# Decoder layers on one Trainium2 core: one run of sums with v per batch, and moved transposes

## The chip, the cores and the metric

The kernel runs on one core of a Trainium2 chip. A core has a matrix engine (TensorE, "PE" in the profile, its weight loads "PEld"), a vector engine (VectorE, "DVE"), a scalar engine (ScalarE, "ACT"), a general engine (GpSimd, "POOL") and an engine that issues DMAs (SyncE, "SP"). Each engine works through its own list of instructions in order and waits on semaphores for the others. [...] The metric is the device time of one execution in microseconds (us). The kernel before has a median of 1778.74 us over three runs, from 1775.16 to 1784.4.

## The reference, cut to what matters

The input `x` is 8 batches of 256 positions of 256 numbers. Six post-norm decoder layers with causal linear attention (16 heads of 16) come first; a cross-attention with a difference of two softmaxes and a three-cycle gated FFN follow. The change touches only the six layers:

```python
for l in range(N_LAYERS):
    q = (x @ Wq[l] + bq[l]).reshape(Bx, Lx, N_HEADS, dh)
    k = (x @ Wk[l] + bk[l]).reshape(Bx, Lx, N_HEADS, dh)
    v = (x @ Wv[l] + bv[l]).reshape(Bx, Lx, N_HEADS, dh)
    a = causal_linear_attn(feature_map(q), feature_map(k), v)
    a = a.reshape(Bx, Lx, dm) @ Wo[l] + bo[l]
    x = x + a
    y = x = layer_norm(x, g1[l], be1[l])
    y = jax.nn.gelu(y @ W1[l] + b1[l], approximate=False) @ W2[l] + b2[l]
    x = layer_norm(x + y, g2[l], be2[l])
```

`feature_map` is `elu + 1`. Written out, the attention is, for each head, the masked product of scores `q k^T` with v (`x` is flipped, so in the original order a query sees the keys at and after its own position), divided by the sum of the masked scores.

## The kernel before, in words

Every batch and layer is cut into four stages, each a Python generator. `stage_q` transposes the batch's `x` (`to_T`), splits it into a high and a low part (`xTh` by ScalarE, `xTl` by VectorE), and projects q, k and v. Each product is made of three passes (high by high, high by low, low by high), six matmuls of 128x256 for each half of an output (`mm3`). The two halves of q are written to the two halves of one PSUM tile, `ps[:, m, :]`, and after each half ScalarE reads it out with the bias (L436); k likewise; v is read by VectorE when both halves are there (L453).

`stage_s` makes the scores. Its first round takes keys of the first 128 positions for all heads, its second and third rounds (`m` = 0 and 1, eight heads each) the keys of the last 128 positions. Each score matmul uses 32 rows of the array, and four of them run beside each other. VectorE masks the first round while reading it out (L505); ScalarE copies the others to `stk` (L521) and POOL masks those (L524). The sums with v (`av`) then use 128 rows and 17 columns: 16 values and one column of ones, which gives the denominator. Four heads are placed on four column groups of the array. One `av(m, ...)` is 16 calls of `mm`, which the trace shows as 32 matmuls. Before, `av` for `m` = 0 and for `m` = 1 are two separate runs into the same bank `av_bank`, each read out by ScalarE (L512) before the next may begin. The result is transposed back (L533) and divided (L537, L538).

`stage_w` projects the attention output, adds the residual and normalizes (`affine`, L345 and L351 on VectorE). `stage_f` transposes `xr` again and runs the FFN: four pieces of W1 with GELU on ScalarE (L596), their split into high and low parts, four pieces of W2.

PSUM has a tag for each purpose: `q` with four banks, `h` with two, `o` and `av` with one each. A new tile of a tag waits for the readers of the tile that had its bank.

The order of the work is written out by hand through due times. A stage yields a number before each step: its due time, in units of one batch (G is a sixteenth of it). `run_tasks` keeps all stages in a heap and runs the step that is due first, so one batch's steps come between those of others. A new batch starts each unit; stages start at `T_S`, `T_W` and `T_F` after it. The lists `Q_T`, `S_T`, `S_F`, `W_T` and the number `X_T` hold the due times inside a stage. `mm` and `tp` chain every TensorE instruction to the one before (`follow("pe", ...)`), so TensorE runs in exactly the order of due times. On the other engines a planner with a timeline of its own places the instructions, bound by data and by a few chains (`follow("dm", ...)`). Weight loads are issued on SP four weights ahead, and VectorE splits each loaded weight into two parts (`wprep`, L216 and L217) in the stage of the last batch of a layer.

Of the kernel before, what the change touches and what calls it, by code (L numbers as in the profile page):

```python
# [30 lines left out]
G = 1 / 16  # L31
T_S = 11.58 * G
T_W = 24.5 * G
T_F = 34 * G
Q_T = (2.6 * G, 3 * G, 4 * G, 5 * G, 6 * G, 7 * G, 7.6 * G, 8.2 * G, 8.8 * G)
S_T = (0.0, 2.02 * G, 6.06 * G, 5.0 * G, 7.12 * G)
S_E = 0.9 * G
S_F = (9.92 * G, 10.52 * G, G)
U_O = (1.5, 2.0, 5.0)
U_B0 = 10.0  # L40
UH = 7.4
# [11 lines left out]
FFP = 3.1  # L53
F_O = (1.45, 2.0, 2.85, 7.6, 11.4, 14.5)
W_T = (3.12 * G, 4.5 * G, 5.5 * G, 8 * G)
X_T = 1.58 * G
F_P = 0.16
W_P = 1
M_W = 1
# [34 lines left out]
def decoder_kernel(ctx: ExitStack, tc: tile.TileContext, A, out, nlay=NLAY, groups=GROUPS):  # L94
# [42 lines left out]
    def mm(o, **kw):  # L137
        ins = pe.matmul(o, **kw)  # L138
        if ORD:
            follow("pe", ins)  # L140
# [140 lines left out]
    def b2col(l, c):  # L281
        return bcol[:, 48 + l * 2 + c:49 + l * 2 + c]

    def bocol(l, c):
        return bcol[:, 60 + l * 2 + c:61 + l * 2 + c]
# [135 lines left out]
    def stage_q(w, b, k, last):  # L421

        l = w % nlay
        yield X_T
        xh, xl = yield from to_T(xr[b], None if w == 0 and b in groups[0][:3] else lambda c: bocol(l, c), t0=X_T)
        yield Q_T[0]
        xs = [(xh[:, c, :], xl[:, c, :]) for c in range(2)]
        q2 = S("stq", [P, 2, 2, 256], F32, 4)
        kf = T2("kf", 5)
        us_, es = (q2[:, 0], kf), []  # L430
        for a, kind in enumerate("qk"):
            wh, wl = W[kind, w, 0]
            ps = PS()
            for m in range(2):
                mm3(ps[:, m, :], [(wh[:, c, half(m)], wl[:, c, half(m)]) for c in range(2)], xs)
                act.activation(us_[a][:, m, :], ps[:, m, :], AF.Identity, bias=bqk1[:, a, l, m:m + 1])  # L436
                yield Q_T[1 + 2 * a + m]
            if last:
                wprep(kind, w + 1)
            e = T2("qe", 2)  # L440
            act.activation(e, us_[a], AF.Relu, scale=-1.0, bias=one)
            es.append(e)
        wh, wl = W["v", w, 0]
        ps = PS()
        va = vaug[k % 3]
        for t in range(2):
            mm3(ps[:, t, :], [(xh[:, c, half(t)], xl[:, c, half(t)]) for c in range(2)],
                [(wh[:, c, :], wl[:, c, :]) for c in range(2)], late="w")
            yield Q_T[5 + t]
        for a in range(2):  # L450
            table_op(act.activation(es[a], es[a], AF.Exp, scale=-1.0))  # L451
        vr = gb["v", w].rearrange("p t (h m) -> p t h m", m=16)
        dve.tensor_tensor(va[:, :, :, 0:16], ps.rearrange("p t (h m) -> p t h m", m=16), vr, ALU.add)  # L453
        if last:
            wprep("v", w + 1)
            rload("v", w + 1)
        yield Q_T[7]
        follow("dm", dve.tensor_tensor(es[0], es[0], us_[0], ALU.max))
        for e in range(2):
            pool.tensor_scalar(q2[:, e], es[0], eo[:, e:e + 1], 1.0, ALU.mult, ALU.mult)  # L460
        yield Q_T[8]
        follow("dm", dve.tensor_tensor(kf, kf, es[1], ALU.max))
        st[b] = dict(v=va, q=q2, k=kf)
# [12 lines left out]
    def stage_s(w, b, k):  # L476
# [1 line left out]
        d = st[b]  # L478
        va, q2, kf = d["v"], d["q"], d["k"]
        avs = S("avs", [P, 4, 256])  # L480
        o = av_bank

        def scores(o4, m, jt):
            n = 256 if jt else P
# [1 line left out]
                r = slice(32 * g, 32 * g + 32)  # L486
                mm(o4[g].rearrange("p (e n) -> p e n", e=2), lhsT=kf[r, m, half(jt)], rhs=q2[r, :, m, 0:n], start=True, stop=True)

        def av(m, a1, a0):
            for s in range(2):  # L490
                for jt in (1, 0):
                    for c in range(4):
                        g, e, n = 2 * s + c // 2, c % 2, 256 if jt else P
                        r = a1[g // 2][:, g % 2, e, :] if jt else a0[g][:, m, half(e)]
                        mm(o[32 * c:32 * c + 17, s, 0:n], lhsT=va[:, jt, 8 * m + 4 * s + c, :], rhs=r,
                           start=jt == 1, stop=jt == 0, tile_position=(0, 32 * c))

        yield S_T[0]
# [5 lines left out]
        for g in range(4):  # L504
            follow("dm", dve.tensor_tensor(a0[g].rearrange("p m (e n) -> p (m e) n", e=2), ps[g].rearrange("p m (e n) -> p (m e) n", e=2), maskT4, ALU.mult))  # L505
        a1s = []

        def second(m):
            yield S_T[2 + 2 * m]
            av(m, a1s[m], a0)  # L510
            yield S_T[2 + 2 * m] + S_E
            act.activation(avs[:, 2 * m:2 * m + 2, :], o, AF.Identity, bias=epc)  # L512

        for m in range(2):
            yield S_T[1 + 2 * m]
            ps = [PS("q") for g in range(4)]
            scores([flat(p) for p in ps], m, 1)
            yield S_T[1 + 2 * m] + S_E
            a1 = [S("stk", [P, 2, 2, 256], F32, 4) for i in range(2)]
            for g in range(4):  # L520
                act.copy(a1[g // 2][:, g % 2], ps[g])  # L521
            for g in range(4):
                x = a1[g // 2][:, g % 2, :, P:256]
                pool.affine_select(x, x, [[0, 2], [-1, P]], ALU.is_ge, 0.0, base=0, channel_multiplier=1)  # L524
            a1s.append(a1)
        for m in range(2):
            yield from second(m)
        ot = T2("hf", 3)
        for t in range(2):
            yield S_F[0] + S_F[2] * t  # L530
# [33 lines left out]

    def stage_f(w, b, k, last):
        l = w % nlay
        xh, xl = yield from to_T(xr[b], lambda c: b2col(l, c), "h")
        xs = [(xh[:, c, :], xl[:, c, :]) for c in range(2)]
        hs = {}
        order = [(1, 0), (1, 1), (1, 2), (2, 0), (1, 3), (2, 1), (2, 2), (2, 3)]  # L570
# [641 lines left out]
```

## Time and profile before

| | |
|---|---|
| median of three runs | 1778.74 us |
| profiled execution | 1775.11 us, span 1773.4 us |
| mean granted clock of TensorE | 0.988 |
| busy: PE / DVE / ACT / POOL | 1689.7 / 1288.3 / 1176.3 / 832.2 us |
| matmuls `p_av<-stk,vaug` (128 rows, 17 columns, 256 moving) | 1536, 387 ns each |
| score copies L521 on ACT | 384, 599 ns each |
| q and k reads L436 on ACT | 192, 475 ns each |
| transposes of xr into p_q / p_h | 224 / 216, 279 and 287 ns in the mean of the layers' form |

A line of the timeline gives the start, the length of a merged group of like instructions, the engine, the line of the code, the operation with its output and inputs, and the number of instructions; square brackets hold idle time before it and what ended that. Matmuls overlap, so the cost of a group is read from its start to the start of the next group and not from its length. An idle time is shown only where the engine's record is empty; a matmul that is held while the one before it still drains shows as a longer distance between starts. Groups are by tile: `p_q<-xTh,wah` is a projection of q or k, `p_q<-wah,xTh` one of v, `p_av<-stk,vaug` sums with v of the last 128 keys, `p_av<-a,vaug` of the first 128, `p_o<-w2h,hh` the second FFN matrix, `p_q<-stq,kf` scores.

### The profile page before, as it was taken

To read this page: it belongs to the slowest core of one execution; us is meant where nothing else is said; L and a number is where in the kernel's file an instruction comes from. 1 tells how busy PE (TensorE), PEld (TensorE's weight loads), DVE (VectorE), ACT (ScalarE), POOL (GpSimd) and SP (SyncE) were. 2 spreads that over 40 slices of the span, in tenths; PEclk is the share of its full clock that TensorE was granted. 3 is DMA by queue.
4 is the path that set the end of the run, shared out by engine and by line. 5 is a ranking of instruction groups with operands and counts; after the bars stand their busy time and mean duration, and the time that the engine had idled before them with its cause. 6 is when DMAs were issued, how large, how long until landed. Compare 5 with 4: busy or idle time off the path is not lost.

```text
span 1773.4 us, 38405 instructions
## 1 busy us (share of the span) xinstructions
PE 1689.7 (95%) x14992; PEld 1345.6 (76%) x14992; DVE 1288.3 (73%) x2846; ACT 1176.3 (66%) x2300; POOL 832.2 (47%) x1295
## 2 busy tenths in 40 slices
PE   6999999999999999999999999999988899999897
PEld 4688887888878888888888887888866555554795
DVE  5566777767777678766787677876668899886586
ACT  3556665666666766666666666666655788877687
POOL 7344444344434444443434434444556666643453
PEclk8999999999999999999999999999999999999998
DMA  4000001000010001100011001100013354440001
GB/s 153 10 1 2 22 19 49 1 1 23 29 38 1 2 22 37 31 1 1 22 37 42 2 1 40 32 10 1 16 41 83 113 135 114 122 125 15 1 1 48
DMA packets 63262, 64.23 MB, mean 36 GB/s; under 512 B 10261, under 2 KB 56600, under 8 KB 63082
## 3 DMA queue, kind: packets, MB, share of 16 engines
q1 hardware_dynamic: 62058, 61.51, 12.2%
q8 instruction: 118, 1.93, 0.4%
q0 software_dynamic: 1024, 0.28, 0.1%
q14 instruction: 62, 0.51, 0.1%
HBM read 49.67 MB, written 11.81 MB: 35 GB/s over the span
## 4 chain that ended last, share of the span: by engine, by line
PE 71%; DVE 12%; ACT 6%; POOL 5%; issue 3%; DMA 1%; SPq 0%; ACTq 0%; POOLq 0%; DVEq 0%
PE p_q L138 24%; PE p_h L138 18%; PE p_o L138 13%; PE p_av L138 10%; PE p_q L143 4%; PE p_h L143 2%; DVE nm L836 2%; DVE a L505 2%; POOL stk L524 1%; POOL hl L579 1%; DVE hh L576 1%; DVE bst L317 1%; POOL nz L295 1%; ACT hf L596 1%; ACT L451 1%
## 5 line engine op out<-in xcount | busy, mean ns | idle before, releaser
L596 ACT ACTIVATE hf<-p_h,bcol 128x256 f32<-128x256 f32 x384 | 161.4, 475 | 211.1 <-PE p_h L138 210.5
L524 POOL TENSOR_SCALAR_AFFINE_SELECT stk<-stk 128x256 f32<-128x256 f32 x384 | 172.9, 476 | 234.7 <-ACT stk L521 231.4
L579 POOL TENSOR_TENSOR hl<-hf,hh 128x512 fp32r<-128x512 f32 x144 | 195.2, 1356 | 160.6 <-DVE hh L576 132.0
L138 PE MATMUL p_q<-stq,kf 32*128 32x512 f32 (+2 forms) x1664 | 245.1, 512 | 11.0 <-ACT wraw L867 1.9
L521 ACT COPY stk<-p_q 128x512 f32<-128x512 f32 x384 | 198.6, 599 | 82.7 <-PE p_q L138 82.5
L294 POOL TENSOR_SCALAR nv<-bmv 128x2 f32<-128x2 f32 x128 | 34.2, 267 | 325.8 <-DVE bmv L319 305.4
L138 PEld LDWEIGHTS p_o<-w2h,hh 128*128 128x128 f32 x768 | 117.2, 189 | 73.4 <-issue 71.9
L138 PE MATMUL p_h<-xTh,w1h 128*128 128x256 f32 x768 | 167.8, 300 | 1.3 <-DVE xTl L392 1.0
L138 PE MATMUL p_o<-w2h,hh 128*128 128x256 f32 x768 | 167.4, 299 | 0.8 <-DVE xr L614 0.8
L138 PE MATMUL p_h<-xTl,w1h 128*128 128x256 f32 x768 | 154.5, 283 | 0.7 <-DVE xTl L392 0.7
L138 PE MATMUL p_h<-xTh,w1l 128*128 128x256 f32 x768 | 154.1, 282 | 0.0
L138 PE MATMUL p_o<-w2h,hl 128*128 128x256 f32 x768 | 151.6, 278 | 0.0
L138 PE MATMUL p_o<-w2l,hh 128*128 128x256 f32 x768 | 151.2, 278 | 0.0
L505 DVE TENSOR_TENSOR a<-p_q,maskT 128x512 f32<-128x512 f32 x192 | 119.1, 681 | 42.2 <-PE p_q L138 42.2
L836 DVE TENSOR_REDUCE nm<-p_q 128x2 f32<-128x512 f32 x189 | 125.0, 677 | 22.6 <-PE p_q L138 21.9
L345 DVE SCALAR_TENSOR_TENSOR xr<-xr,bmv,gb 128x256 f32<-128x256 f32 x192 | 133.6, 733 | 0.0
L138 PE MATMUL p_av<-stk,vaug 128*17 128x256 f32 x1536 | 126.8, 387 | 5.2 <-POOL stk L524 4.2
L138 PEld LDWEIGHTS p_h<-xTh,w1h 128*128 128x128 f32 x768 | 118.8, 191 | 3.7 <-issue 2.6
L138 PEld LDWEIGHTS p_h<-xTh,w1l 128*128 128x128 f32 x768 | 119.4, 191 | 0.0
L138 PEld LDWEIGHTS p_h<-xTl,w1h 128*128 128x128 f32 x768 | 118.5, 190 | 1.1 <-DVE xTl L392 1.1
L138 PEld LDWEIGHTS p_o<-w2h,hl 128*128 128x128 f32 x768 | 116.7, 188 | 0.0
L138 PEld LDWEIGHTS p_o<-w2l,hh 128*128 128x128 f32 x768 | 116.6, 188 | 0.0
(355 smaller groups left out, 4552.0 us busy)
## 6 DMA issues: line engine op xcount, KB each, us to landing
wraw<-in_L_attn_W_dram SPq DMA_DIRECT2D x48, 256.0 KB
xq<-pc SPq DMA_DIRECT2D x16, 384.0 KB
xk<-pc SPq DMA_DIRECT2D x16, 192.0 KB
stq<-xq SPq DMA_DIRECT2D x16, 192.0 KB
stk<-xq SPq DMA_DIRECT2D x16, 192.0 KB
xr<-in_x_dram SPq DMA_DIRECT2D x8, 256.0 KB
px<-in_x_dram SPq DMA_DIRECT2D x8, 256.0 KB
cx<-in_ctx_dram SPq DMA_DIRECT2D x16, 128.0 KB
```

The costliest lines, as they stand in the source:

```text
L138: ins = pe.matmul(o, **kw)
L143: ins = pe.transpose(*a)
L294: pool.tensor_scalar(v, var, 1e-5, 1.0, ALU.add, ALU.mult)
L295: pool.tensor_tensor(z, v, mhalf, ALU.pow)
L317: dve.bn_stats(st[:, t, :], y[:, t, :])
L345: dve.scalar_tensor_tensor(y[:, t, :], y[:, t, :], mv[:, t, 0:1], g[:, t, :], ALU.subtract, ALU.mult)
L505: follow("dm", dve.tensor_tensor(a0[g].rearrange("p m (e n) -> p (m e) n", e=2), ps[g].rearrange("p m (e n) -> p (m e) n", e=2), maskT4, A ...
L521: act.copy(a1[g // 2][:, g % 2], ps[g])
L524: pool.affine_select(x, x, [[0, 2], [-1, P]], ALU.is_ge, 0.0, base=0, channel_multiplier=1)
L579: (pool if M_L >> j & 1 else dve).tensor_tensor(hl, hs[j], hh, ALU.subtract)
L596: table_op(act.activation(hf[:, m, :], ps[:, m, :], AF.Gelu, bias=b1col(l, 2 * j + m)))
L836: dve.tensor_reduce(nm[:, s, 2 * h:2 * h + 2], ps, AX.X, ALU.max)
```

## The change

The two runs of sums become one. Both `av` calls now stand at one due time, one behind the other. The run for `m` = 0 writes to a bank of tag `q`, the run for `m` = 1 to `av_bank`, and both banks are read out after that. The bank of tag `q` holds what earlier tiles left in it, so the run for `m` = 0 takes 32 columns of v (17 of its own and 15 that belong to the next heads); the rows above 17 are not used afterwards. In the list `S_T` the two due times of the runs become one, 8.12 sixteenths, where they were 6.06 and 7.12.

The transposes at the head of `stage_q` are due at 0.4 sixteenths (before: 1.58) and use the tag `h` (before: `q`). The transposes at the head of `stage_f` are due 1.9 sixteenths after the stage's start (before: at its start). The due times of the halves of q, k and v in `Q_T` change, and the second output transposes are due half a sixteenth after the first (before: a whole one).

```diff
-Q_T = (2.6 * G, 3 * G, 4 * G, 5 * G, 6 * G, 7 * G, 7.6 * G, 8.2 * G, 8.8 * G)
-S_T = (0.0, 2.02 * G, 6.06 * G, 5.0 * G, 7.12 * G)
+Q_T = (2.0 * G, 2.3 * G, 4.1 * G, 4.3 * G, 4.5 * G, 6.5 * G, 7.6 * G, 8.2 * G, 8.8 * G)
+S_T = (0.0, 2.02 * G, 8.12 * G, 5.0 * G)
-S_F = (9.92 * G, 10.52 * G, G)
+S_F = (9.92 * G, 10.52 * G, 0.5 * G)
-X_T = 1.58 * G
+X_T = 0.4 * G
+H_T = 1.9 * G
@@ stage_q
-        xh, xl = yield from to_T(xr[b], None if w == 0 and b in groups[0][:3] else lambda c: bocol(l, c), t0=X_T)
+        xh, xl = yield from to_T(xr[b], None if w == 0 and b in groups[0][:3] else lambda c: bocol(l, c), "h", t0=X_T)
@@ stage_s
-        o = av_bank
-        def av(m, a1, a0):
+        def av(o, m, a1, a0):
+            n_out = 17 if m else 32
+            flat_v = va.rearrange("p t h n -> p (t h n)")
-                        mm(o[32 * c:32 * c + 17, s, 0:n], lhsT=va[:, jt, 8 * m + 4 * s + c, :], rhs=r,
+                        i = 17 * (16 * jt + 8 * m + 4 * s + c)
+                        mm(o[32 * c:32 * c + n_out, s, 0:n], lhsT=flat_v[:, i:i + n_out], rhs=r,
                            start=jt == 1, stop=jt == 0, tile_position=(0, 32 * c))
-        def second(m):
-            yield S_T[2 + 2 * m]
-            av(m, a1s[m], a0)
-            yield S_T[2 + 2 * m] + S_E
-            act.activation(avs[:, 2 * m:2 * m + 2, :], o, AF.Identity, bias=epc)
+        yield S_T[2]
+        os_ = (PS("q"), av_bank)
         for m in range(2):
-            yield from second(m)
+            av(os_[m], m, a1s[m], a0)
+        yield S_T[2] + S_E
+        for m in range(2):
+            act.activation(avs[:, 2 * m:2 * m + 2, :], os_[m], AF.Identity, bias=epc)
@@ stage_f
-        xh, xl = yield from to_T(xr[b], lambda c: b2col(l, c), "h")
+        yield H_T
+        xh, xl = yield from to_T(xr[b], lambda c: b2col(l, c), "h", H_T)
```

## The prediction

> **What bounds the kernel now.** I read the page's busy shares and clock row first, then the windows, then the timelines of TensorE and ScalarE through one quiet period, because the shares alone cannot say which wait ends last.
>
> ```profile
> span 1773.4 us, 38405 instructions
> ...
> PE 1689.7 (95%) x14992; PEld 1345.6 (76%) x14992; DVE 1288.3 (73%) x2846; ACT 1176.3 (66%) x2300; POOL 832.2 (47%) x1295
> ...
> PEclk8999999999999999999999999999999999999998
> ```
>
> TensorE is busy 95% of the span at nearly the full clock; nothing else passes 76%. A period (one batch through one layer) is the distance between the first score rounds of two batches, 733.05 and 759.69 in the timeline:
>
> ```profile
> 733.05:759.69 26.64, 26.64 (x262) 22.80 (x261) 18.12 (x40) 17.66 (x34) 11.31 (x18) 1.00 0.01 2
> ```
>
> The columns are length, then busy time of PE, PEld, DVE, ACT, POOL, then clock, DMA share and GB/s. PE is busy for all 26.64 us and no other engine for over 18.12 (weight loads aside, which run beside matmuls). A layer is eight such periods; starts read from the timeline give 26.63 in four of them, 26.73 to 27.3 in three, and about 31 in the one where the last batch's weights are prepared. So every microsecond that PE loses in a period is lost 46 to 48 times. Now PE inside that period:
>
> ```profile
> 742.73 0.60 PE L143 MATMUL p_q<-ident,xr 128*128 128x128 f32 x4
> 743.26 0.63 PE L138 MATMUL p_av<-stk,vaug 128*17 128x256 f32 x8
> 743.71 0.40 PE L138 MATMUL p_av<-a,vaug 128*17 128x128 f32 x8
> 743.93 0.61 PE L138 MATMUL p_av<-stk,vaug 128*17 128x256 f32 x8
> 744.36 0.40 PE L138 MATMUL p_av<-a,vaug 128*17 128x128 f32 x8
> 744.69 0.66 PE L143 MATMUL p_h<-ident,xr 128*128 128x128 f32 x4
> ...
> 750.11 0.40 PE L138 MATMUL p_q<-xTl,wah 128*128 128x256 f32 x2
> 750.35 0.40 PE L138 MATMUL p_h<-xTh,w1h 128*128 128x256 f32 x2
> ...
> 750.83 0.40 PE L138 MATMUL p_h<-xTl,w1h 128*128 128x256 f32 x2
> 751.08 0.51 PE L138 MATMUL p_q<-xTh,wah 128*128 128x256 f32 x2
> 751.42 0.40 PE L138 MATMUL p_q<-xTh,wal 128*128 128x256 f32 x2
> ```
>
> Durations overlap, so cost is read from start to start: six 128x256 matmuls take 0.72 (749.63 to 750.35). Two things matter. The run of sums is a block of 1.43 with a fixed price at both ends. And the second half of k's projection (751.08) does not follow its first half (last pair at 750.11): six matmuls of the FFN stand between, and even so PE starts 0.05 after ScalarE has finished reading the first half:
>
> ```profile
> 742.03 2.05 ACT L521 COPY stk<-p_q 128x512 f32<-128x512 f32 x4 [1.33 <-PE p_q L138]
> 743.94 0.88 ACT L386 ACTIVATE xTh<-p_q,bcol 128x256 fp32r<-128x256 f32 x2
> ...
> 748.27 0.69 ACT L512 ACTIVATE avs<-p_av,epc 128x512 f32<-128x512 f32 x1 [0.98 <-PE p_av L138]
> ...
> 750.55 0.47 ACT L436 ACTIVATE kf<-p_q,bqk 128x256 f32<-128x256 f32 x1 [0.17 <-PE p_q L138]
> ```
>
> 750.55 plus 0.475 is 751.02. In every batch after the ramp that I read, over 40, this distance is 0.05. Both halves of a projection share one PSUM bank (L433, halves `ps[:, m, :]`), and the second half waits for the reader of the first. Where nothing stands between, at the start of the run, the bare wait shows:
>
> ```profile
> 22.60 0.40 PE L138 MATMUL p_q<-xTl,wah 128*128 128x256 f32 x2
> 23.56 0.50 PE L138 MATMUL p_q<-xTh,wah 128*128 128x256 f32 x2 [0.56 <-ACT stq L436]
> 23.91 0.40 PE L138 MATMUL p_q<-xTh,wal 128*128 128x256 f32 x2
> ```
>
> The last matmul of the first half starts at 22.72, the second half at 23.56: 0.84 where back to back is 0.12. That is 0.72 lost, and the first pair then takes 0.35 instead of 0.24, another 0.11.
>
> **The change part by part.** I put TensorE's new order together from the due times modulo one period (in sixteenths): q's transposes 0.4, FFN 0.56, last scores 0.58, FFN 1.56, q first half 2.0, q second half 2.3, FFN 2.56 and 3.56, both sums 3.7, xr's transposes 3.9, k 4.1 and 4.3, v 4.5, FFN 4.7, output transposes 5.5 and 6.0, v 6.5. The same working gives the order of before exactly as its timeline shows it. It follows that q's two halves now stand next to each other (before, the second run of sums stood between them), and k's two as well (before, FFN matmuls).
>
> *One run of sums.* Before, 740.07 to 756.36 is 16.29. From the same pieces the new order is 14 groups of six at 0.71, 9.94; the score round with its ends 0.09 + 1.07 + 0.10; q's transposes 0.36 + 0.08; sums 0.09 + 1.30 + 1.43; xr's transposes 0.41 + 0.08; two output transposes 0.88: 15.83. The difference is 0.46, of which 0.11 is the end of k's wait, booked below. Saved: 0.35 a period, all on the path. The 32 columns of the first run (17 before) cost between nothing and 0.1: matmuls still last as long as their 256 moving columns, and weight loads of 32 columns take 109 ns against 97 to 99 in this trace. I take nothing, the loads being covered by 0.43 of streaming.
>
> *q's second half waits.* From the score round's start: scores 1.07, FFN 0.81, q's first half 0.71, so it ends at 2.59 and its read could start at 2.79 (0.20 later, as 750.35 to 750.55). But ScalarE starts the four score copies 1.16 after the scores and needs 1.91 for them (742.03 to 743.94), until 3.07. The read starts 0.28 late: 0.72 + 0.28 + 0.11 = 1.11. Behind the waiting matmul stands all of PE; nothing can pass it. The bounds are 0.83 (ScalarE free) and 1.6 (one more read of 0.48 ahead of it).
>
> *k's second half waits.* From the end of the sums: ScalarE has the second evacuation from 0.14, then the two casts of xr's transposes from 0.74 to 1.57 (start 0.72 after the transposes, as 744.69 to 745.41). k's first half runs from 0.41 to 1.20 and could be read at 1.40; it is read at 1.57, 0.17 late. Lost 0.72 + 0.17 + 0.11 = 1.00, less the 0.11 that before already pays: 0.89. Bounds 0.72 and 1.5 (both evacuations in front).
>
> *Moved steps.* xr's transposes come 1.9 sixteenths (3.2 us) later and no longer wait for the layer norm; q's come 1.18 earlier, into a bank of tag h, and their low part is no longer behind weight preparation. In the long periods:
>
> ```profile
> 497.35 0.89 PE L143 MATMUL p_h<-ident,xr 128*128 128x128 f32 x4 [0.58 <-DVE xr L351]
> ...
> 500.61 0.77 PE L138 MATMUL p_q<-xTl,wah 128*128 128x256 f32 x2 [1.21 <-DVE xTl L392]
> ```
>
> Against the quiet period these places lose 0.85 and 1.64, and the period ahead 0.62: 3.1, five times in the run. What is late next is DVE's own backlog; k's weight preparation (two casts, 1.1 us, and one weight load on SP) moves from 6.0 to 4.5, in front of xr's low part. I take back 0.6 for it and count 2.5 each, 12 in all; ends 0 and 20. The SP load is four weights ahead of use, so it is hidden; with that cover gone it would cost its landing once a layer. No POOL instruction is added or reordered: its selects are done before the sums, which now come later. The final transposes stand about 3.9 behind the end of the sums, after 0.7 of evacuation.
>
> *Sum.* A period changes by -0.35 + 1.11 + 0.89 = +1.65. The first two batches already have bare pairs, so 46 times: +76. Less 12: +64. The profiled execution took 1775.1 (span 1773.4 and 1.7 around it), 3.6 under the median of 1778.7; 1839 and 1843 follow, and I say 1840. The cross-attention and the last FFN, after about 1330, keep their order.
>
> [...]
>
> **The rivals.**
> 1. *Only one pair is bare.* If one wait were covered by something I misplaced, a period changes by 0.89 - 0.35 = 0.54 or 0.76: +25 to +35 less 12, at 1788 to 1802. Against it: no other PE step has a due time between either pair.
> 2. *ScalarE becomes a second bound.* Its reads are placed by a planner whose estimates the trace does not show; with the upper ends 1.6 and 1.5 a period costs +2.75, 126 in all, 1890 or more. Against it: 17.66 busy of 26.64.
> 3. *Faster: the pairs do not wait.* If PE wrote the second half while ScalarE reads the first, 0.46 a period and 12 go: 1742. It decides as soon as both waits together cost under 0.35 + 0.26 (12 over 46), 0.61 a period. Against it: the bare pair above loses 0.83 alone.
>
> **How the numbers follow.** My forecast (own range 1805 to 1880) has 0.80, rival 1 0.06, rival 2 0.08, rival 3 0.06. The lower bounds give -0.35 + 0.83 + 0.72 = +1.20 a period, 55 less 20, about 1810; delays on ScalarE halfway to the upper bounds give +2.2, 101 less nothing, about 1880. The range 1797 to 1880 holds both and the upper part of rival 1. Half a per cent, 9 us, is about what a measurement tells from no change. Faster 0.06, same 0.03 (the weak end of rival 1), slower 0.91.
>
> **What would show it.** Quiet periods near 28.3 instead of 26.63; waits of p_q on ACT stq and kf at L436 of about 0.7 to 1.2, some 46 each, in the chain of waits; one block of 64 sums matmuls; no wait of p_h's transposes on DVE xr. It would be wrong if the second halves start 0.12 after the first, or if a period stays under 27.

## The result, and the profile after

The changed kernel takes 1962.4 us in the median of four runs (1959.4 to 1963.7), against 1779.3 for the kernel before on the same chip (four runs, 1775.2 to 1784.4): a ratio of 1.102, with a 95% interval of 1.0995 to 1.1045. The forecast was 1840, with a range up to 1880. The sign was right; the loss of 183 us is three times the forecast 61.

From the page of the changed kernel, whose profiled execution took 1961.6 us:

```profile
span 1959.7 us, 38315 instructions
...
PE 1769.6 (90%) x14992; PEld 1403.3 (72%) x14992; DVE 1280.6 (65%) x2846; ACT 1179.4 (60%) x2300; POOL 827.2 (42%) x1295
...
PEclk8999999999999999999999999989989989999998
```

The number of matmuls is the same (14992), but TensorE is busy 80 us more and idle 106 us more. Idle time was foreseen, longer matmuls were not. They are the visible side of the clock row, which has slices at 8: the mean granted clock fell from 0.988 to 0.957. Groups of two 128x256 matmuls start 0.24 apart at full clock in the changed kernel (839.31 and 839.55) and 0.43 apart where the granted clock is 0.50 (808.27 and 808.70).

TensorE's waits in the changed kernel (engine, tile and line that waits, what it waited for: us in total, times, longest):

```profile
PE p_q L139 <- DVE xTl L393: 50.1, 39, 3.4
PE p_q L139 <- ACT kf L437: 29.9, 48, 1.1
PE p_q L139 <- ACT stq L437: 27.2, 47, 0.9
PE p_q L139 <- ACT stk L518: 15.9, 6, 4.9
PE p_q L139 <- DVE rb L550: 10.5, 38, 0.3
PE p_q L139 <- POOL stq L461: 5.9, 11, 1.4
```

The second and third lines are the two waits that the prediction added, in the place and the number that it gave. The first line is the largest, and the prediction had no term for it: the low part of q's input comes late. The wait for `DVE rb` (the low part of the attention output) in the score round has grown too: the kernel before has 1.7 us of it, in 7 waits. `rb` reads a bank of tag `q`, the tag that the scores write.

Now TensorE through one period of the changed kernel, from its timeline (start, length of a merged group, engine, line, operation, count, idle before and what ended it):

```profile
825.46 0.71 PE L139 MATMUL p_q<-stq,kf 32*128 32x256 f32 x6
826.46 1.12 PE L139 MATMUL p_q<-stq,kf 32*128 32x256 f32 x10 [0.29 <-DVE rb L550]
...
833.16 0.60 PE L144 MATMUL p_h<-ident,xr 128*128 128x128 f32 x4
...
836.54 0.40 PE L139 MATMUL p_q<-xTh,wal 128*128 128x256 f32 x2
837.63 0.78 PE L139 MATMUL p_q<-xTl,wah 128*128 128x256 f32 x2 [0.70 <-DVE xTl L393]
838.97 0.50 PE L139 MATMUL p_q<-xTh,wah 128*128 128x256 f32 x2 [0.56 <-ACT stq L437]
...
841.28 0.64 PE L139 MATMUL p_q<-stk,vaug 128*32 128x256 f32 x8
...
844.02 0.66 PE L144 MATMUL p_h<-ident,xr 128*128 128x128 f32 x4
...
844.99 0.40 PE L139 MATMUL p_q<-xTl,wah 128*128 128x256 f32 x2
846.00 0.51 PE L139 MATMUL p_q<-xTh,wah 128*128 128x256 f32 x2 [0.61 <-ACT kf L437]
```

Four stops are to be seen in order: inside the score round (826.46), in the middle of q's first half (837.63, its high-part matmuls are at 836.54), before q's second half (838.97) and before k's second half (846.00). The sums are one block of 2.74 us, 841.28 to 844.02. No transpose waits on `xr`.

What ScalarE (`xTh`), POOL (`nz`) and VectorE do ahead of the second stop, same kernel and period:

```profile
833.80 0.84 ACT L387 ACTIVATE xTh<-p_h,bcol 128x256 fp32r<-128x256 f32 x2
...
835.29 0.70 POOL L296 TENSOR_TENSOR nz<-nv,mhalf 128x2 f32<-128x2 f32 x1
...
832.54 1.89 DVE L346 SCALAR_TENSOR_TENSOR xr<-xr,bmv,gb 128x256 f32<-128x256 f32 x2
836.03 1.15 DVE L352 SCALAR_TENSOR_TENSOR xr<-xr,nz,rowf 128x256 f32<-128x256 f32 x2 [1.59 <-POOL nz L296]
837.11 0.86 DVE L393 SCALAR_TENSOR_TENSOR xTl<-p_h,bcol,xTh 128x256 fp32r<-128x256 f32 x2
```

q's low part (L393) stands in VectorE's queue behind the last step of a layer norm (L352). That step waits 1.59 us for POOL's `nz`, which ends at 835.99. VectorE runs nothing meanwhile, and the low part, whose operand `xTh` is ready at 834.64, starts at 837.11.

The layers make 47 distances from one batch's first score round to the next. I account over 32 of these periods (the second to the fifth layer), where no ramp is. The windows of the kernel before and after over these 32 periods, with length, busy time of PE, PEld, DVE, ACT and POOL, clock, DMA share and GB/s; first before:

```profile
219.00:1099.00 880.00, 870.78 (x8338) 734.64 (x8334) 640.70 (x1360) 567.84 (x1059) 370.66 (x548) 1.00 0.07 20
```

and after:

```profile
255.00:1264.60 1009.60, 920.82 (x8336) 768.85 (x8335) 639.07 (x1360) 569.71 (x1060) 369.02 (x546) 0.97 0.06 18
```

The same matmuls take 129.3 us more, of which PE's records show 50 as busy time. Over all 47 periods the loss is 180.9 us (1303.3 to 1484.2), so practically all of it is in the layers, as forecast.

The table gives, for each kernel run, the time of the 32 periods and its parts. They are worked out from starts of matmuls in the trace: "q pair" and "k pair" are the time by which the second half starts later than 0.12 after its first half, where the two stand next to each other; "low" the same for the first low-part matmul of q; "scores" is the time from the first matmul of the first score round to the next operation (all of it, not an excess); "slow clock" is the time by which other steps are longer than the same kernel's median while the granted clock is at half; "at half" is the time at half clock itself. Each ratio is against the kernel before on the same chip, whose medians lie between 1778.6 and 1779.8, so kernels from different chips can be compared; E1 to E4, E8 and E10 to E12 have two runs each, the others four or more.

| kernel | median us | ratio, 95% | 32 periods | q pair | k pair | low | scores | slow clock | at half |
|---|---|---|---|---|---|---|---|---|---|
| before | 1779.3 | 1 | 880.3 | 0 | 0 | 2.2 | 49.1 | 0 | 0 |
| after | 1962.4 | 1.0995–1.1045 | 1009.6 | 27.3 | 24.6 | 42.6 | 63.8 | 31.4 | 68.3 |
| E1 q halves apart | 1909.9 | 1.0649–1.0821 | 976.7 | 0 | 24.5 | 49.2 | 63.6 | 12.3 | 30.7 |
| E2 q late | 1882.3 | 1.0515–1.0646 | 948.9 | 24.6 | 24.5 | 11.6 | 63.7 | 10.1 | 17.1 |
| E3 waits filled | 1930.3 | 1.0784–1.0916 | 988.9 | filled | filled | filled | 63.8 | 7.4 | 17.1 |
| E4 v later | 1945.5 | 1.0868–1.1003 | 1004.7 | 28.2 | 24.6 | 42.8 | 49.1 | 50.6 | 112.6 |
| E5 merged, halves apart | 1801.6 | 1.0099–1.0138 | 889.1 | 0 | 0 | 13.2 | 48.7 | 7.2 | 10.2 |
| E6 E5, old q transposes | 1828.1 | 1.0252–1.0313 | 911.6 | 0 | 0 | 17.1 | 48.8 | 11.1 | 17.1 |
| E7 q transposes alone | 1776.3 | 0.9969–0.9999 | 880.1 | 0 | 0 | 0.5 | 49.3 | 1.3 | 3.4 |
| E8 filled, other bank | 1932.6 | 1.0827–1.0891 | 986.7 | filled | filled | filled | 64.1 | 6.1 | 13.7 |
| E9 k halves further apart | 1802.2 | 1.0094–1.0139 | 889.2 | 0 | 0 | 13.4 | 64.6 | 6.4 | 10.2 |
| E10 only k halves apart | 1953.5 | 1.0953–1.1 | 1013.4 | 27.3 | 0 | 49.8 | 63.7 | 45.5 | 112.6 |
| E11 old due times | 1871.6 | 1.0494–1.0539 | 946.9 | 26.2 | 0 | 24.5 | 48.8 | 11.9 | 20.5 |
| E12 layer norm behind | 1872.1 | 1.0487–1.0551 | 948.3 | 31.6 | 24.4 | 5.1 | 64.0 | 7.7 | 17.1 |
| E13 E5, Relu behind | 1782.5 | 1.0004–1.0028 | 878.3 | 0 | 0 | 13.5 | 48.8 | 9.5 | 13.7 |
| E14 E13 and E12 | 1757.5 | 0.9859–0.9892 | 858.2 | 0 | 0 | 0 | 48.8 | 0 | 0 |

For the change itself: 27.3 + 24.6 + 40.4 (low) + 14.7 (scores) + 31.4 (slow clock), and 4.1 of a wait on POOL's `stq` just ahead of the score round (eight times, by starts), make 142.5; less 0.35 times 32 for the merged run, 11.2, that is 131.3 where 129.3 was measured. The sum closes to within 2 us, but a sum that closes names places, not causes; the experiments test these.

### The profile page after: what moved, and what is told of

The parts are those of the page before. It is cut to its first block, busy times and chain, and to the rows that moved or that the text cites. A ratio compares the mean times of both kernels' runs of the same rounds, so it can differ in the third digit from the quotient of the medians.

```text
span 1959.7 us, 38315 instructions
## 1 busy us (share of the span) xinstructions
PE 1769.6 (90%) x14992; PEld 1403.3 (72%) x14992; DVE 1280.6 (65%) x2846; ACT 1179.4 (60%) x2300; POOL 827.2 (42%) x1295
## 3 DMA queue, kind: packets, MB, share of 16 engines
q1 hardware_dynamic: 62058, 61.51, 11.1%
## 4 chain that ended last, share of the span: by engine, by line
PE 34%; ACT 16%; DVE 12%; POOL 5%; issue 3%; DMA 0%; ACTq 0%; SPq 0%; POOLq 0%; DVEq 0%
PE p_q L139 16%; PE p_h L139 7%; PE p_av L139 5%; PE p_o L139 4%; ACT hf L599 2%; ACT stk L518 2%; ACT L599 2%; ACT L452 2%; ACT xTh L387 2%; DVE nm L839 2%; POOL stk L521 2%; POOL nz L296 1%; DVE a L508 1%; ACT qe L452 1%; PE p_q L144 1%
## 5 line engine op out<-in xcount | busy, mean ns | idle before, releaser
L139 PE MATMUL p_q<-stq,kf 32*128 32x512 f32 (+2 forms) x1664 | 258.3, 523 | 20.4 <-DVE rb L550 10.5
L139 PE MATMUL p_o<-w2h,hh 128*128 128x256 f32 x768 | 178.4, 316 | 0.8 <-DVE xr L617 0.8
L139 PEld LDWEIGHTS p_o<-w2h,hh 128*128 128x128 f32 x768 | 128.1, 206 | 69.9 <-issue 68.3
L139 PE MATMUL p_o<-w2l,hh 128*128 128x256 f32 x768 | 161.1, 293 | 0.0
L139 PE MATMUL p_q<-xTh,wah 128*128 128x256 f32 x384 | 98.5, 340 | 67.9 <-ACT kf L437 29.9
L139 PE MATMUL p_q<-xTl,wah 128*128 128x256 f32 x384 | 98.5, 325 | 51.0 <-DVE xTl L393 50.1
L617 DVE TENSOR_TENSOR xr<-p_o,xr 128x512 f32<-128x512 f32 x48 | 33.2, 691 | 150.0 <-PE p_o L139 150.0
L139 PEld LDWEIGHTS p_q<-stq,kf 32*128 32x128 f32 x1536 | 83.6, 186 | 63.4 <-DVE rb L550 26.6
L139 PEld LDWEIGHTS p_o<-w2l,hh 128*128 128x128 f32 x768 | 127.4, 204 | 0.0
L139 PEld LDWEIGHTS p_q<-xTh,wah 128*128 128x128 f32 x384 | 61.9, 203 | 91.1 <-ACT kf L437 39.8
```

What stands on the lines that cost most here:

```text
L617: dve.tensor_tensor(y, acc, y, ALU.add)
```

## The experiments

The theory after the result: two bank waits as forecast, a third wait behind a layer norm, and a clock that is lowered by the idle time of all of them. The rival: the waits are worth what their idle time is, and nothing more, so that the slow matmuls would not go with them. The diffs below are against the changed kernel unless said otherwise; `Q_T` is in sixteenths `G`.

### E1: q's halves apart

```diff
-Q_T = (2.0 * G, 2.3 * G, 4.1 * G, 4.3 * G, 4.5 * G, 6.5 * G, ...
+Q_T = (2.0 * G, 3.0 * G, 4.1 * G, 4.3 * G, 4.5 * G, 6.5 * G, ...
```

> The changed kernel with one due time altered: q's second half at 3.0 sixteenths, so that six FFN matmuls stand between q's halves again; k's halves stay next to each other. Bank theory: the wait for the reader of q's first half (0.81 a period in the changed kernel's trace) is covered, 46 times 0.81 = 37 us, so 1925 us, and less if TensorE then also keeps its full clock for longer. Rival, that VectorE's queue sets the pace: the wait only moves to the next place that needs VectorE, and the time stays within 10 us of 1962.

Measured: 1909.9 us, 52 less than the changed kernel. The wait of q's second half is gone from the table (27.3 to 0), the low part's wait has grown by 6.6, and slow matmuls cost 12.3 instead of 31.4. So the wait is real and of the size read; removing it also gave back 19.1 of slow clock, 0.7 times as much as the wait itself. (27.3 less 6.6 plus 19.1 is 39.8; the 32 periods became 32.9 shorter, the rest is in no column.)

### E2: both of q's halves late, still next to each other

```diff
-Q_T = (2.0 * G, 2.3 * G, 4.1 * G, ...
+Q_T = (3.6 * G, 3.65 * G, 4.1 * G, ...
```

> The changed kernel with both halves of q at 3.6 and 3.65 sixteenths, behind two more groups of six FFN matmuls; the halves still stand next to each other. Queue theory: q's low part is late because it stands in VectorE's queue behind the last step of the layer norm, so q's first half, 1.4 us later, meets it ready in most periods: the 1.3 a period goes, 46 times that is 61 us, about 1900 us, less with a steadier clock. The wait between q's halves stays at 0.7 to 1.1. Rival, that the low part is late because q's transposes themselves are late or ScalarE is: it would be later in step with TensorE and the time would stay near 1962.

Measured: 1882.3. The pair's wait stays (24.6), the low part's falls from 42.6 to 11.6, the slow clock from 31.4 to 10.1. The low part is late only for the place at which the change needs it.

### E3 and E8: the waits filled with useless matmuls

Eight extra matmuls stand between the high and low part of q's first half, and five behind the first halves of q and of k. Here is E3:

```diff
+    def idle_fill(n, l, r):
+        for _ in range(n):
+            mm(av_bank[:, 0, :], lhsT=l, rhs=r, start=True, stop=True)
...
+            if i == 4:
+                idle_fill(mid, order[0][0], order[0][1])
...
+                if m == 0:
+                    idle_fill(5, wh[:, 0, half(0)], xs[0][0])
```

In E3 the five matmuls behind k's first half overwrite part of the sums of `m` = 1 before they are read out, so that part of the output is replaced. E8 is the same with the fill of k written into the bank that v takes next:

```diff
+                    vps = PS() if a else None
+                    idle_fill(5, wh[:, 0, half(0)], xs[0][0], vps if a else av_bank)
...
-        ps = PS()
+        ps = vps
```

> The changed kernel with extra matmuls of 128x256 that no one reads, in the places where TensorE waits: five behind each first half of q and of k, eight in front of the low pass of q's first half. All waits stay; TensorE is only kept busy in them. Clock theory: the 127 us at half clock beyond those of before come from the idle time, so they go, and with them about half as much time: 1962 less 50 is about 1912 us, with more work done. Rival, that the granted clock has nothing to do with these gaps: the time stays at 1962 or rises by the extra matmuls that the waits do not cover (up to 18 times 0.12, 2 us a period, 90 us).

> The run with extra matmuls again, the five behind k's first half now written to the bank that v takes next, so that they touch no sum that is still to be read. Clock theory: as there, little half clock in the layers, and the time 25 to 45 us under the changed kernel, 1917 to 1937 us. Rival, that the earlier gain came from the overwritten sums: no gain, 1962.

Measured: 1930.3 and 1932.6 us. E8 issues some 1700 instructions more than the changed kernel and is 30 us faster. The clock row of E8's page:

```profile
span 1928.2 us, 40042 instructions
...
PEclk8999999999999999999999999999998999999998
```

In the 32 periods E8 is 22.9 us shorter, and its slow-clock column 25.3 shorter (31.4 to 6.1). Nothing was removed from the work; TensorE was only kept from standing idle. That the idle time lowers the clock here (the mean granted clock is 0.980 in E8 and 0.957 in the changed kernel), and that this costs at least about 30 us of the 183, is shown by this pair.

### E4: the first half of v back behind the FFN

```diff
-Q_T = (2.0 * G, 2.3 * G, 4.1 * G, 4.3 * G, 4.5 * G, 6.5 * G, ...
+Q_T = (2.0 * G, 2.3 * G, 4.1 * G, 4.3 * G, 5.8 * G, 6.5 * G, ...
```

> The changed kernel with v's first half back behind the first FFN matmuls (5.8 sixteenths instead of 4.5). Theory: because v came forward, the first FFN piece and all that ScalarE does behind it (GELU, two table loads, the exponentials, the cast before the output projection) stand 0.7 nearer to the next score round, which then waits for that cast's low part: 0.5 a period, 46 times, 25 us, so about 1937 us. Rival, that the score round waits for POOL's product of q, which does not depend on v's place: no gain, 1962.

Measured: 1945.5. The score round is back at 49.1 of 63.8, so its delay came from v standing ahead of the first FFN piece: ScalarE's block of GELU, exponentials and the cast of `num` hangs on that piece, and `rb` on the cast. But 14.7 us less delay made the 32 periods only 4.9 shorter, since the slow clock rose from 31.4 to 50.6. The clock row of E4's page:

```profile
PEclk8999998999999998999989999989999999999998
```

TensorE is idle for less time in all (78 us in the 32 periods, against 89 in the changed kernel) and longer at half clock (112.6 us against 68.3): in these two kernels it counts where the idle time lies, not only how much there is.

### E10: only k's halves apart

```diff
-Q_T = (2.0 * G, 2.3 * G, 4.1 * G, 4.3 * G, ...
+Q_T = (2.0 * G, 2.3 * G, 3.0 * G, 4.3 * G, ...
```

> The changed kernel with only k's first half moved to 3.0 sixteenths, in front of the last FFN group and the sums, so that k's halves are apart; q's stay next to each other. Bank theory: the wait for the reader of k's first half, 0.81 a period, goes: 37 us, about 1925 us, and 10 to 20 less if the clock recovers as it did when q's halves were taken apart (1910 us). Rival, that q's waits take over: within 10 us of 1962.

Measured: 1953.5. k's wait is gone (24.6 to 0) and the 32 periods are 3.8 us longer. TensorE's waits in E10:

```profile
PE p_q L139 <- DVE xTl L393: 56.4, 40, 4.1
PE p_q L139 <- ACT stq L437: 26.8, 47, 0.9
```

Quiet periods read 30.67 to 30.70, and in nearly every one the clock falls for one stretch of 3.41 us. Windows of E10 set on the edges of such a stretch (columns as above):

```profile
642.73:646.14 3.41, 2.06 (x13) 1.46 (x12) 1.52 (x4) 1.55 (x4) 1.71 (x4) 1.00 0.00 0
646.14:649.55 3.41, 3.41 (x18) 3.41 (x17) 0.00 (x0) 1.67 (x3) 0.00 (x0) 0.50 0.02 5
649.55:652.97 3.42, 3.42 (x72) 2.34 (x70) 2.44 (x7) 0.97 (x2) 1.16 (x2) 1.00 0.00 0
```

In the first, TensorE is idle for 1.35 us of 3.41. In the second it is never idle, and runs 18 matmuls at a clock of 0.50. In the third it runs 72. The clock that is lost here follows an idle time of 1.35 us, well under one stretch. The forecasts of E4 and E10 from waits alone fall with this.

### E11: the change with the old list of q, k and v

```diff
-Q_T = (2.0 * G, 2.3 * G, 4.1 * G, 4.3 * G, 4.5 * G, 6.5 * G, ...
+Q_T = (2.6 * G, 3 * G, 4 * G, 5 * G, 6 * G, 7 * G, ...
```

> The changed kernel with q's, k's and v's due times of before, everything else of the change kept. k's halves and v are as before; q's halves are still next to each other, because the run of sums that stood between them has moved. Theory: of the losses only q's wait (0.8 a period) and part of the wait for the low part (0.7 of 1.3) stay, less 0.35 saved: 46 times 1.2 is 53 us over before, about 1832 us, and up to 1850 with some half clock. Rival, that the list of due times is innocent and the merged run costs the time: near 1962.

Measured: 1871.6. k's wait and the delay of the scores are gone, q's wait is not (26.2): between 2.6 and 3 sixteenths only the second run of sums stood before, and the merge has taken it away. So q's wait comes from the merged run as such, and k's wait and the scores' delay from the new list.

### E12: the layer norm behind the low part

The last layer-norm step gets a due time of its own, and is chained on VectorE behind q's low part.

```diff
+            if late is not None:
+                yield late
...
+                    if late is not None:
+                        follow("lnq", ins)
...
+                if chain:
+                    follow("lnq", ins)
...
-        yield from affine(y, gb["1", w], gb["f", w], M_W, W_T[3])
+        yield from affine(y, gb["1", w], gb["f", w], M_W, W_T[3], 9 * G)
```

> The changed kernel with the order of two steps on VectorE exchanged: q's low part is put in front of the last step of the layer norm after the attention (and that step's due time set behind it); nothing else moves. Queue theory: the low part waited only for its turn, so the wait of 1.3 a period goes, about 60 us and some half clock, as when q's halves were moved behind more FFN matmuls (1882 us): 1880 to 1905 us. Rival, that the low part is late for ScalarE's cast or the transposes: the wait stays, 1962.

Measured: 1872.1, 90 us less than the changed kernel. TensorE's waits in E12 (its lines are 4 to 6 further down):

```profile
PE p_q L139 <- ACT stq L443: 37.3, 47, 0.9
PE p_q L139 <- ACT kf L443: 29.7, 48, 1.1
...
PE p_q L139 <- DVE xTl L397: 5.9, 5, 1.4
```

and ScalarE in one of its periods:

```profile
727.45 2.05 ACT L524 COPY stk<-p_q 128x512 f32<-128x512 f32 x4 [0.92 <-PE p_q L139]
729.36 0.51 ACT L443 ACTIVATE stq<-p_q,bqk 128x256 f32<-128x256 f32 x1
```

The wait on `xTl` falls from 50.1 to 5.9, in the 32 periods from 42.6 to 5.1, and 23.7 of slow clock go with it. q's own wait grows from 27.2 to 37.3, since its first half now ends while ScalarE is still at the score copies: ScalarE reads it right behind them, without a pause. That is the case the prediction had priced. No work changed, only the order of two steps in VectorE's queue; ScalarE and POOL run theirs in the same order as in the changed kernel in all 32 periods. This shows the third wait's cause.

### E5, E6, E7: the merged run alone

E5 has the one run of sums and the moved transposes of q and `xr`, as the change does, but keeps something between the halves of both projections:

```diff
-Q_T = (2.0 * G, 2.3 * G, 4.1 * G, 4.3 * G, 4.5 * G, 6.5 * G, ...
+Q_T = (3.6 * G, 3.9 * G, 4.1 * G, 5.0 * G, 6 * G, 7 * G, ...
-S_F = (9.92 * G, 10.52 * G, 0.5 * G)
+S_F = (9.92 * G, 10.52 * G, G)
-H_T = 1.9 * G
+H_T = 1.65 * G
```

> The changed kernel's merged sums, its q transposes and its banks, with the other due times so that nothing is bare: q's first half at 3.6 (behind two more FFN groups), xr's transposes at 3.65 in front of the sums, q's second half at 3.9 behind the sums, k at 4.1 and 5.0 with FFN matmuls between, v at 6.0 and 7.0, output transposes a whole sixteenth apart as before. Theory: all four losses go and the merged run's saving shows, 0.35 a period less than before's 26.63: quiet periods of 26.3, 46 times 0.35 = 16 us under before, about 1763 us, and the clock as before. Rival, that merging saves nothing: 1779; or that merging itself costs, for the sums' readouts come too late: over 1790.

Measured: 1801.6, ratio 1.0119. Still slower than before, with both pairs apart. TensorE and ScalarE in one period of E5; TensorE first:

```profile
646.20 0.40 PE L139 MATMUL p_h<-xTh,w1h 128*128 128x256 f32 x2
...
647.33 0.51 PE L139 MATMUL p_q<-xTh,wah 128*128 128x256 f32 x2 [0.26 <-ACT kf L437]
```

and ScalarE:

```profile
645.68 0.48 ACT L437 ACTIVATE stq<-p_q,bqk 128x256 f32<-128x256 f32 x1 [0.19 <-PE p_q L139]
646.19 0.72 ACT L442 ACTIVATE qe<-stq,one 128x512 f32<-128x512 f32 x1
646.82 0.45 ACT L437 ACTIVATE kf<-p_q,bqk 128x256 f32<-128x256 f32 x1
```

k's first half is ready for reading at about 646.4, 0.2 after the FFN matmul behind it starts at 646.20. ScalarE reads it only at 646.82, since q's Relu (L442, 0.72) is ahead of it. That costs 0.41 a period, more than the merged run saves. E13 takes this up. The 32 periods account for 8.8 of E5's 22 us over the kernel before; 11.8 lie in the last layer.

E6 is E5 with q's transposes where they were before (`X_T` 1.58, tag `q`); E7 is the kernel before with only that part of the change:

```diff
-X_T = 1.58 * G
+X_T = 0.4 * G
-        xh, xl = yield from to_T(xr[b], ..., t0=X_T)
+        xh, xl = yield from to_T(xr[b], ..., "h", t0=X_T)
```

> The same as the run with nothing bare, but q's transposes as before the change: at 1.58 sixteenths behind the last score round, in a bank of tag q. Theory: q's first half comes 2.0 behind the transposes' end, which is near the time that the two casts and the low part need, so up to 0.5 a period is lost against the run with the early transposes, 0 to 23 us, and 1763 to 1786 us. Rival, that the transposes' place is free of cost: within 4 us of the run with the early transposes.

> The kernel before with only q's transposes moved to 0.4 sixteenths and to tag h. Theory: the transposes no longer stand next to the run of sums, which cost 0.07 to 0.17 a period at that place, and their casts are never late: 3 to 8 us less than before, 1771 to 1776 us. Rival, that the low part in VectorE's queue then delays the layer norm, or that a bank of tag h is missed: slower than before.

Measured: 1828.1 for E6, 26.5 more than E5; 1776.3 for E7, within half a per cent of before. In E6's quiet periods (27.47 against 26.81), TensorE reaches q's first half 1.85 us after q's transposes, and 0.58 of the 0.66 is lost inside that first half, on its inputs. With the runs of sums apart the place of the transposes makes hardly any difference; once they are one, and with the due times of E5, the early place is needed.

### E9 and E13: k's first half read earlier, or needed later

E9 is E5 with k's second half one FFN piece later (the first diff is against E5), E13 is E5 with ScalarE's Relu of q chained behind its read of k's first half:

```diff
E9
-Q_T = (3.6 * G, 3.9 * G, 4.1 * G, 5.0 * G, ...
+Q_T = (3.6 * G, 3.9 * G, 4.1 * G, 5.6 * G, ...
E13
+                rd = act.activation(us_[a][:, m, :], ps[:, m, :], AF.Identity, bias=bqk1[:, a, l, m:m + 1])
+                if a == 1 and m == 0:
+                    follow("kr", rd)
+                    es.append(T2("qe", 2))
+                    follow("kr", act.activation(es[0], us_[0], AF.Relu, scale=-1.0, bias=one))
...
```

> The run with nothing bare, with k's second half at 5.6 sixteenths instead of 5.0, so that two groups of FFN matmuls and the output transposes stand between k's halves. In the run before, k's second half still waited 0.5 a period, because ScalarE had both readouts of the sums, q's second half and q's Relu in front of k's first half. Theory: this goes, and quiet periods fall from 26.81 to about 26.3, under the 26.63 of the kernel before, so that the saving of the merged run shows; 46 times 0.5 is 24 us, 1778 us. Rival, that merging saves nothing: quiet periods no shorter than 26.6, and about 1790 us.

> The run with nothing bare, with one step on ScalarE put behind another: q's Relu comes after the readout of k's first half. The due times are those of that run. Theory: the 0.4 to 0.5 a period that k's second half waited there goes, and nothing else moves: quiet periods of 26.3, 0.35 under the 26.63 of the kernel before, as the merged run's two saved ends say; against 1802 us that is 46 times 0.5, 23 us, 1779 us. Rival, that the merged run saves nothing in time because another wait takes the room, as the score round did when k's second half was moved instead: quiet periods of 26.6 or more and 1795 us or more.

Measured: 1802.2 for E9, the same as E5: k's wait is gone and the score round takes 64.6 instead of 48.7, about what was gained (15.9 against 0.41 times 32, 13.1). ScalarE in one period of E9:

```profile
592.48 0.63 ACT L452 ACTIVATE qe<-qe 128x512 f32<-128x512 f32 x1
593.02 0.46 ACT L437 ACTIVATE kf<-p_q,bqk 128x256 f32<-128x256 f32 x1
593.57 0.72 ACT L442 ACTIVATE qe<-kf,one 128x512 f32<-128x512 f32 x1
```

The read of k's second half and its Relu now stand between the two exponentials (L452), inside ScalarE's block of GELU, exponentials and the cast of `num`; in E5 both stand ahead of that block. From the block's first GELU to the cast it takes 6.67 here and 5.33 in E5, and the score round waits for `rb` again (8.6 us in 36 waits, 0.2 in E5). E13: 1782.5, level with before to 0.16%. Its quiet periods are 26.33 to 26.43, shorter than before's 26.63, and its 32 periods are 2.0 us shorter in all. They still lose in the long period of a layer, 31.5 to 32.2 us against 31.0 to 31.5, where the low part waits (13.5 in the 32 periods), and the last layer is 11.5 us longer than before's.

### E14: E13 with the layer norm behind the low part

The edits of E13 and E12 together.

> The same, and q's low part in front of the last step of the layer norm on VectorE, as in the run that exchanged those two. Theory: quiet periods as there, 26.3, and the waits for the low part that are left in the long periods (about 13 us in the run with nothing bare) go with their half clock: 10 to 18 us less, 1762 to 1770 us, under the kernel before. Rival, that the layer norm's step, now later, delays xr's transposes in the long periods: no less than the other run.

Measured: 1757.5 us in the median of four runs (1754.9 to 1760.3), ratio 0.9876 with an interval of 0.9859 to 0.9892: 1.2% under the kernel before. Windows of three quiet periods of E14, columns as above:

```profile
529.49:555.89 26.40, 26.40 (x262) 22.95 (x261) 17.92 (x40) 17.71 (x34) 11.19 (x18) 1.00 0.01 1
555.89:582.20 26.31, 26.31 (x261) 22.87 (x261) 17.99 (x40) 17.68 (x34) 11.29 (x18) 1.00 0.01 2
582.20:608.61 26.41, 26.41 (x262) 22.96 (x261) 17.91 (x40) 17.69 (x34) 11.19 (x18) 1.00 0.01 2
```

TensorE is busy for all of it, at full clock. VectorE in the second of these, where the low part (L397 here) now precedes the layer norm's last step:

```profile
564.40 0.88 DVE L397 SCALAR_TENSOR_TENSOR xTl<-p_h,bcol,xTh 128x256 fp32r<-128x256 f32 x2
565.95 1.16 DVE L354 SCALAR_TENSOR_TENSOR xr<-xr,nz,rowf 128x256 f32<-128x256 f32 x2 [0.67 <-POOL nz L296]
```

The quiet period is 26.37 in the mean of these three against 26.63 before: 0.26 of the 0.35 that the merged run was said to save. The long period of each layer is 28.3 to 28.6 where it was 31.0 to 31.5. Together 22.1 us in the 32 periods. The 0.35 was added up for the order of the changed kernel; E14 has other neighbours around the sums (xr's transposes ahead of them, q's second half behind), and what makes the difference of 0.09 was not tested.

## Why the prediction was right in sign and wrong in size

*The merged run.* Right: 0.35 a period forecast, 0.26 seen in E14, where nothing else hides it. The block of sums itself takes 2.74 in the changed kernel (841.28 to 844.02), where 1.30 and 1.43 were added up.

*q's second half.* The mechanism, the place and the number of waits (47 for "some 46") were right; the size was 0.85 (27.3 over 32) where 1.11 was taken. The term that was off is the 0.28 of ScalarE being busy with score copies. In the changed kernel the low part makes q's first half end so late that ScalarE has been idle for 0.83 by then, and the bare wait of 0.72 and the 0.11 remain. E12 shows the priced case: with the low part in time, the pair costs 0.99 (31.6 over 32).

*k's second half.* Right: 0.77 for 0.89, 48 waits. ScalarE reads k's first half right behind the casts of the transposes, as worked out:

```profile
844.16 0.69 ACT L529 ACTIVATE avs<-p_av,epc 128x512 f32<-128x512 f32 x1 [0.61 <-PE p_av L139]
844.75 0.83 ACT L387 ACTIVATE xTh<-p_h,bcol 128x256 fp32r<-128x256 f32 x2
845.46 0.48 ACT L437 ACTIVATE kf<-p_q,bqk 128x256 f32<-128x256 f32 x1
```

These are ScalarE's lines of the changed kernel; 845.46 plus 0.48 is 845.94, and TensorE resumes at 846.00.

*Moved steps: the step that failed.* It said of q's transposes that "their low part is no longer behind weight preparation", and took back 12 us. It looked at what the low part leaves, and not at what it now stands behind. q's first half had come to 2.0 sixteenths, where TensorE is ready for the low part soon after a layer norm's last step gets its numbers from POOL (at about 836.8 and at 835.99 above), and VectorE's order has the low part behind that step. That costs 1.26 a period (40.4 over 32), in place of a gain of 0.26 (12 over 46), and with the clock that goes with it 90 us of the 183 (E12). The sentence "No POOL instruction is added or reordered" holds for the number (1295 in both pages), not in every period for the order (at 643.88 of the changed kernel `nv` and `nz` run ahead of `hl`, at 739.78 of the kernel before behind it), and is beside the point: POOL's `nz` was off the path, and became part of it when an instruction that the path needs was queued behind its reader. The waits that should go did go (no transposes wait on `xr`), but the sum above closes without a gain from them: the two longest periods of a layer take 34 to 36 us in the changed kernel, where they were 27 and 31.

*v's earlier place.* The prediction put v at 4.5 and "FFN 4.7" behind it, and did not ask what hangs on that FFN piece. It is ScalarE's block ahead of the scores: 0.46 a period, 0.13 more with POOL's `stq`. E4 and E11 remove it.

*The clock.* It was not a term at all. In the kernel before, TensorE was idle for at most 1.2 us in any stretch of 3.41 us of these periods, counted on the grid of the last section, and the clock was full. In the changed kernel the loss is 0.98 a period (31.4 over 32), and E8 shows that the cause is idle time: with the waits filled 6.1 of the 31.4 are left. The two waits that the prediction forecast would hardly have brought it: they lie 7 us apart (838.97 and 846.00), and E2 and E12, which keep both, lose 10.1 and 7.7. It comes with the low part's wait, 1.3 us ahead of q's (837.63 and 838.97): of the 16 full-clock stretches that a half-clock one follows, 15 hold a wait for the low part, 13 of them with q's wait beside it. So most of this loss too goes back to the step that failed (23.7 of the 31.4 in E12).

By periods: -0.35 + 0.85 + 0.77 + 1.26 + 0.46 + 0.13 + 0.98 = 4.10, measured 4.04 (129.3 over 32); forecast -0.35 + 1.11 + 0.89 less 0.26 = 1.39. Of the difference of 2.65 (2.71 by the terms), the low part is 1.52, the clock 0.98, the scores with POOL's `stq` 0.59; the two bank waits came out 0.38 smaller. The three terms that the forecast had right in kind come to 1.27 a period, 58 us in 46.

*The rivals.* That only one pair is bare (1788 to 1802) did not happen: both were. That the pairs do not wait did not either. "ScalarE becomes a second bound" named 1890 or more and was nearest in time, but by another mechanism: ScalarE's reads were, if anything, earlier than priced. The range failed because no case in it had a new wait on VectorE, nor a clock below full.

*Open.* Why VectorE's list has the layer norm first was only read from the trace: the planner that places it works with its own estimates. The split between "low" and "slow clock" is not sharp, since part of a wait can itself be at half clock: in the changed kernel the wait of 0.56 on ACT `stq` that ends at 807.68 runs past 807.46, where a half-clock stretch begins.

## What to carry to other kernels

For every step that is needed earlier, read what stands ahead of its inputs in the queue of each engine that makes them, at the new time: here VectorE, busy for 65% of the span, still held q's low part up behind an instruction that waited 1.59 us for POOL. Count the new idle time of TensorE by stretches of a few microseconds and not only in the sum, for in the 32 periods of the changed kernel half clock followed all 15 stretches of 3.41 us with 1.34 us or more of idle time, and in E1 taking away a wait of 27.3 us gave back another 19. And take an expected gain apart from its company: here the merged run was worth 0.26 us a period once its neighbours kept out of the way, and what came with it cost 4.

## What the runs showed of the hardware

In the clock records of all sixteen traces the half-clock stretches begin and end on one grid of 3.413 us; in the 32 periods of the changed kernel there are 16 of them, 12 of 3.41 us and 4 of 6.83. The table gives TensorE's idle time inside each full-clock stretch of that grid, over the same 32 periods, by what the next stretch was, for five of the sixteen kernels:

| kernel | idle us, next at half (count) | idle us, next at full (count) |
|---|---|---|
| before | none | up to 1.20 (257) |
| after | 1.27 to 2.64 (16) | up to 1.32 (260) |
| E4 | 1.26 to 2.37 (26) | up to 1.16 (236) |
| E10 | 1.35 to 3.41 (29) | up to 1.50 (235; three above 1.30) |
| E14 | none | up to 0.53 (251) |

In the changed kernel the idle time ahead of half clock was in one piece (2.43 us in the stretch from 1053.22) or in two (0.78 and 0.56 in the one from 367.14). The counts do not part the stretches cleanly: of some 4250 full-clock stretches in the sixteen kernels eight stand apart from the rest. After 1.35 to 1.79 us of idle time the clock stayed full six times (three in E10, two in E11, one in E9), and after 0.48 (E9) and 0.96 (E3) it fell; what decides there is open. A whole stretch of idle time was not needed: the one in E10 that is shown above had TensorE busy for 2.06 of 3.41 us, and the next was at half.

In E10 the quiet periods are 30.67 to 30.70 us, nine stretches are 30.72, and 33 stretches in the 32 periods are at half. My estimate from these three numbers is that the same waits fall into the same place of the grid in period after period, and that taking k's wait away gained nothing there for that reason. It was not shown: no kernel with a period shifted on purpose was run.
